# A decoder layer: gathers and loads moved, ACT in written order, last norm's scaling on ACT

## The chip, the cores and the metric

The kernel runs on one core of a Trainium2 chip. Its time is the time on the device in microseconds (us), the median of several executions. The profile is that of one execution. The engines are called TensorE (PE), VectorE (DVE), ScalarE (ACT), GpSimd (POOL) and SyncE (SP) here; SP only issues DMAs, and ACT and POOL issue some beside their other work.

## What is computed

One decoder layer on 32 sequences of 64 tokens with 512 features, all in 32-bit floats. Cut to what matters:

```python
# self-attention: 32 query heads, 8 key/value heads, head size 128
k_sel = k_cache[block_idx].reshape(-1, NKV, HD)          # 512 cached keys
k_full = concatenate([k_sel, k[0]])                      # and 64 new ones
x = layernorm(x + softmax(q @ k_full.T / sqrt(HD)) @ v_full @ wo.T)
# cross-attention: each sequence attends to its own 64 context rows
x = layernorm(x + softmax(q2 @ k2.T * scale) @ v2 @ Wo + bo)
# feed forward: z = x W + b; a low-rank m; gamma limits the norm of m
x = layernorm(x + z + min(0.5 * norm(z) / (norm(m) + 1e-6), 1) * m)
```

The 576 keys and values of the self-attention are the same for all 2048 tokens.

## The kernel before, in words

**Tiles.** The 2048 tokens form four blocks (tb) of 512. `acc[tb]` holds a block's residual, 1 MB, as four pieces of 128 tokens. The larger products (queries, output projection, keys and values of the context) are done with seven products in place of eight: the operands' quarters are first added up (`token_sums`, `output_sums`, `right_sums` on GpSimd, lines 190 to 199 and 256 to 259), and the seven results are read out of three PSUM banks x, y and z in an order given by a list. For the queries, `Queries.step(i)` issues product i on TensorE and puts the reading steps on a list: products 1 and 2 are copied by ACT (L310, L314), 6 and 7 are read by VectorE (L322, L325), and the "corner" quarter c[1, 1] is made of products 5 and 7 (L299, or L302 with a bias).

**Self-attention.** A unit n is one key/value group g, one block tb and one of that group's four heads h; there are 8 x 4 x 4 = 128 units, 16 to a group. r is the unit's number within its group. A unit has four score tiles i of 128 queries by 576 keys. For each, TensorE makes the scores (L615) in one of two PSUM buffers, VectorE takes the maximum (L620), ACT the exponential with its sum (L623), and VectorE inverts the sum (L632), scales (L633) and turns the tile in 32x32 squares (L641). `move` (L653) then rearranges the turned tiles with 16 DMAs, four for each range of 32 partitions. Two units later TensorE multiplies with the values (L661, `values` and `shared_values`), and ACT copies the result to oT (L684). Between the score tiles stand places for one query product of the next block ("q") or one output product of a past block ("w"): `steps` gives them for each h. The first blocks have an order of their own: block 1's query products come as 1, 2, 6, 5, 7, 3, 4, with z and x in the same bank.

**Around a group's change.** `load_group` loads the next group's key and value weights. `gather_keys` and `gather_values` fetch its cached rows, one indirect DMA of GpSimd each for keys and for values, four times in a group: in units r = 4, 5, 6, 7. Each is preceded by a small addition of VectorE (L538). In unit 8 `rotate` applies the rotary angles to the gathered keys: three steps on VectorE's side before the sum (L558 to L560, L562) and two on GpSimd (L557, L561). `new_keys` (matmuls L576, L582) runs in unit 8 and `cached_keys` (transposes L596) in unit 10.

**What sets the order.** A start section is written out for all engines. From there on (line 812) TensorE and VectorE run in the order in which the program names their instructions; for ACT, GpSimd and SP a scheduler of the compiler chooses the order from its own estimate of times. In the cross-attention TensorE, VectorE and GpSimd run in written order, and for the last unit and the feed forward TensorE and GpSimd only.

**Loads of the residual.** At the end of the start section (L797) the four blocks of x are loaded into `acc`, one DMA of 1 MB each, block 0 by SP and the others by ACT.

**Cross-attention.** Its 32 units are a group g and a block tb. For each, the seven query products (L282) come in the order 1, 6, 5, 7, 2, 4, 3. For the last group, g = 7, the norm of a block follows its last output product: `stats` (L149 to L152) at once, and `scale` (reciprocal L155 and four VectorE scalings L157) is put on the list `scales`, which the next unit empties after its query product 1, ahead of the reading of product 6. The list `later` holds the transposes (L129) of the scaled block; they come after query product 2. Block 2's scaling is emptied in the last pass of the loop and block 3's after it, ahead of the feed forward of block 2 (L1172 to L1206).

Of the kernel before, what the change touches and what calls it, by code (L numbers as in the profile page):

```python
# [52 lines left out]
def decoder_layer(  # L53
# [57 lines left out]
    def rows(src, tb):  # L111
        return src[tb * TB : (tb + 1) * TB, :].rearrange("(j p) f -> p j f", p=P)
# [25 lines left out]
        for part in layernorm_parts(tb, name):  # L138
            part()

    def layernorm_parts(tb, name):
        a = acc[tb]
        rstd = small.tile([P, TPB], F32, tag="rstd", name=f"rstd_{name}_{tb}")
        mv = small.tile([P, TPB, 2], F32, tag="mv", name=f"mv_{name}_{tb}")

        def stats():
            for j in range(TPB):
                st = small.tile([P, 6], F32, tag="st", name=f"st_{name}_{tb}_{j}")
                nc.vector.bn_stats(st, a[:, j, :])  # L149
                nc.vector.bn_aggr(mv[:, j, :], st)  # L150
            nc.vector.tensor_scalar_add(rstd, mv[:, :, 1], LN_EPS)
            nc.scalar.activation(rstd, rstd, AF.Sqrt)  # L152

        def scale():
            nc.vector.reciprocal(rstd, rstd)  # L155
            for j in range(TPB):
                nc.vector.tensor_scalar(  # L157
                    a[:, j, :], a[:, j, :], mv[:, j, 0:1], rstd[:, j : j + 1],
                    ALU.subtract, ALU.mult,
                )  # L160

        return stats, scale

    def layernorm_tile(tb, j, name):
        a = acc[tb][:, j, :]
# [123 lines left out]
    class Queries(Product):  # L289
        def __init__(self, left, right, qT, name, tags, bias=None):  # L290
            super().__init__(left, right, name, tags)
            self.c = {(i, j): qT[:, quarter(i, j)[0], quarter(i, j)[1]]
                      for i in range(2) for j in range(2)}
            self.bias = bias

        def final(self, y, i, j):
            c = self.c[i, j]
# [8 lines left out]
        def step(self, i):  # L306
            c = self.c
            assert not self.reads
            if i == 1:
                nc.scalar.copy(c[1, 0], self.mul("x", 1, True))  # L310
            elif i == 2:
                x = self.mul("x", 2)
                if self.bias is None:
                    nc.scalar.copy(c[0, 0], x)  # L314
                else:
                    for m in range(2):
                        nc.scalar.activation(
                            c[0, 0][:, m, :], x[:, m, :], AF.Identity, bias=self.bias[m]
                        )
            elif i == 6:  # L320
                y = self.mul("y", 6, True)
                self.reads.append(lambda: nc.vector.tensor_tensor(c[0, 1], y, c[1, 0], ALU.add))  # L322
            elif i == 7:
                y = self.mul("y", 7)
                self.reads.append(lambda: nc.vector.tensor_tensor(c[1, 1], y, c[1, 0], ALU.add))  # L325
            elif i == 4:
                y = self.mul("y", 4)
                self.reads.append(lambda: self.final(y, 1, 0))
            elif i == 5:
                z = self.mul("z", 5, True)  # L330
                self.corner = lambda: self.final(z, 1, 1)
            elif i == 3:
                z = self.mul("z", 3)
                self.reads.append(lambda: self.final(z, 0, 1))
# [129 lines left out]
    with ExitStack() as ph:  # L464
# [243 lines left out]
        def q_step(n):  # L708

            b = n // REP + 1  # L710
            if b < NB:
                if b not in qrs:

                    start_queries(b, {"x": "q", "y": "w" if b == 1 else "q", "z": "q"})
                    qrs[b].todo = list((1, 2, 6, 5, 7, 3, 4) if b == 1 else ORDER)
                i = qrs[b].todo.pop(0)
                qrs[b].step(i)
                reads.append(qrs[b].read)
                if i in (5, 7) and not {5, 7} & set(qrs[b].todo):
                    reads.append(qrs[b].corner)  # L720

        def w_step(b):
# [70 lines left out]
        nc.vector.tensor_tensor(t[4], q[1, 0], t[2], sub)  # L793
        tok[1] = token_sums(xTs[1], "tx1", nc.gpsimd)
        wo_cur[0] = load_right(woT[columns(0), :], "wo0", nc.gpsimd, first=wo_cur[0])
        for tb in range(NTB):
            (nc.scalar if tb else nc.sync).dma_start(out=acc[tb], in_=rows(x, tb))  # L797

        def last_products(i):
            if i == 3:  # L800
# [8 lines left out]

        begin.close()  # L810

        ph.enter_context(tc.manual_schedule(
            engines={mybir.EngineType.PE, mybir.EngineType.DVE}
        ))

        for n in range(N):
            b, h = divmod(n, REP)
            g, r = units[n][0], n % PER  # L820
            if r == REP and g + 1 < NKV:
                load_group(g + 1)
            if r // REP == 1 and g + 1 < NKV:
                gather_keys(g + 1, h)
            if r == 2 * REP and g + 1 < NKV:
                rotate(g + 1)
                later.append(lambda g=g: new_keys(g + 1))
            if r == 2 * REP + 1 and g + 1 < NKV:
                later.append(lambda g=g: cached_keys(g + 1))
            if n == N - REP:  # L830
                encT[0] = big.tile([P, NC, TB], F32, tag="qT", name="encT0", bufs=2)
                load_features(encT[0], encT_in, 0)
            steps = {0: "qwqw", 1: "qw q", 2: "wqwq", 3: "w qw"}[h]

            def step(place):
                if n < REP:

                    i = {(0, 0): 3, (0, 1): 7, (0, 3): 4}.get((n, place))
                    if i:
                        last_products(i)  # L840
                    elif (n, place) in ((0, 2), (1, 0), (1, 1), (1, 2), (1, 3), (2, 0), (2, 2)):
                        q_step(n)
                elif steps[place] == "q":
                    q_step(n)
                elif steps[place] == "w":
                    w_step(b - 2 if h < 2 else b - 1)
                flush()

            def spare_bank():

                if n % 2 == 0 and later:
                    later.pop(0)()

            scores(n, 0)
            step(0)
            spare_bank()
            scores(n, 1)
            if 0 < n < REP:

                move(n - 1, (3,), nc.scalar)  # L860
            if n >= 2:
                values(n - 2, 0, 2 if n % 2 == 0 else 3)
            step(1)
            scores(n, 2)
            step(2)
            if r // REP == 1 and g + 1 < NKV:
                gather_values(g + 1, h)
            scores(n, 3)
            if n >= 2:
                values(n - 2, 2 if n % 2 == 0 else 3, NKT)  # L870
                if n % 2:
                    shared_values(n - 2)
            step(3)
            spare_bank()
            if h == REP - 1:
                if b + 2 < NB:
                    g2, tb2, _ = units[(b + 2) * REP]
                    if tb2 == 0:
                        wq_cur[g2] = load_left(wqT[:, columns(g2)], f"wq{g2}", nc.gpsimd)
                    tok[b + 2] = token_sums(xTs.pop(b + 2), f"tx{g2}_{tb2}", nc.gpsimd)  # L880
                elif b + 2 == NB:
                    kvw[0] = load_kv_left(0, "wq")
                else:
                    encR[0] = token_sums(encT[0], "te0", nc.gpsimd)
            if h == REP - 1 and b + 3 < NB or n == 0:

                b2 = b + 3 if n else 2
                xTs[b2] = token_room(b2, f"xT{b2}")
                load_features(xTs[b2], xT_in, b2 % NTB)
            move(n, (0, 1, 2) if n < REP - 1 else range(NQD))  # L890

# [44 lines left out]
    with ExitStack() as ph:  # L938
# [200 lines left out]
        def project(n, *steps):  # L1139
            g, tb = units[n]  # L1140
            for i in steps:
                pjs[n].step(i)
                pjs[n].read()
            if steps[-1] == 4:
                del pjs[n]
                if g == NKV - 1:
                    stats, scale = layernorm_parts(tb, "x")
                    stats()
                    scales.append(scale)
                    later.append(lambda: transpose_block(tb, "x2"))  # L1150
# [98 lines left out]
        for n in range(N + 1):  # L1249
# [6 lines left out]
            if n < N:  # L1256
                g, tb = units[n]
                q = queries(n)
                for i in (1, 6, 5, 7):
                    q.step(i)  # L1260
                    q.read()
                    while scales:
                        scales.pop(0)()
                q.corner()
                q.step(2)


                behind = g > 0 and tb == 1
                if not behind:
                    next_tokens(n + 1, 0)  # L1270
# [102 lines left out]
```

## Time and profile before

| | |
|---|---|
| time before, median of 3 runs | 3090.13 us (3086.34 to 3092.24) |
| the profiled execution's own time | 3088.83 us |
| its span, first to last instruction | 3085.9 us |
| TensorE busy | 3034.2 us, 98% of the span |
| VectorE busy | 2186.5 us, 71% |
| ACT busy | 757.2 us, 25% |
| GpSimd busy | 967.6 us, 31% |
| TensorE's mean granted clock | 0.997 |
| self-attention | to about 1870 us |
| keys and values of the context | to about 2053 us |
| cross-attention and feed forward | to the end |

How to read the profile: a line of a timeline gives the start, the duration, the engine, the line of the kernel, the operation, what it writes and reads, how many like it were merged, and in brackets how long the engine was idle before it and what released it. A row of waits gives the engine and line that waited, what it waited for, the total in us, how many times, and the longest. Issuing a DMA is not counted as busy time; SPq, ACTq and POOLq are the issuing sequencers.

### The profile page before, as it was taken

Reading aid. Unit: us, or ns where it says so; the run is one execution under the profiler, and the core shown is the slowest. Engines: PE = TensorE matmul, PEld = TensorE weight load, DVE = VectorE, ACT = ScalarE, POOL = GpSimd, SP = SyncE. Lnnn points to the kernel's source line nnn. Section 1 sums busy time; section 2 is a strip of 40 time slices with the busy share of each in tenths; the row PEclk is TensorE's granted clock in tenths of the full one; section 3 lists DMA queues with packets and bytes.
Section 4 is the critical chain, followed back from the end, with each engine's and each line's share of the span. In section 5 each row is a group of like instructions: output and inputs, shape, how many; then the busy total and the mean of one; then the engine's idle time right before and its main releaser. Section 6 shows DMA issues by size and latency. Waiting matters only on the chain.

```text
span 3085.9 us, 42306 instructions
## 1 busy us (share of the span) xinstructions
PE 3034.2 (98%) x14944; PEld 2320.6 (75%) x14944; DVE 2186.5 (71%) x3957; ACT 757.2 (25%) x1760; POOL 967.6 (31%) x789
## 2 busy tenths in 40 slices
PE   8999999999999999999999999999999999999998
PEld 6777677777777777777777769988888888888764
DVE  6777877877877877877877764436656666666677
ACT  2323232232332232232232221211111111111122
POOL 4221322321321322322322123136444444454421
PEclk9999999999999999999999999999999999999999
DMA  6444444444444444444344343321121121121101
GB/s 210 115 115 119 113 115 122 111 122 114 109 126 115 103 129 113 106 126 115 100 125 112 96 122 138 110 96 52 52 69 49 49 69 49 49 68 49 48 28 41
DMA packets 200913, 298.66 MB, mean 97 GB/s; under 512 B 44160, under 2 KB 94848, under 8 KB 200704
## 3 DMA queue, kind: packets, MB, share of 16 engines
q1 hardware_dynamic: 187328, 282.51, 33.8%
q10 hardware_dynamic: 11328, 9.26, 1.0%
q0 software_dynamic: 2048, 4.20, 0.5%
q8 instruction: 120, 1.97, 0.3%
q14 instruction: 89, 0.73, 0.1%
HBM read 107.05 MB, written 20.97 MB: 41 GB/s over the span
## 4 chain that ended last, share of the span: by engine, by line
PE 91%; DVE 4%; DMA 2%; SPq 2%; ACT 1%; issue 1%; ACTq 0%; DVEq 0%
PE po L661 15%; PE s L615 15%; PE sx L1043 2%; PE pox L1114 2%; PE w_0y L282 1%; PE q_3y L282 1%; PE wx_2y L282 1%; PE wx_1y L282 1%; PE w_3y L282 1%; SPq L653 1%; PE qx_2y L282 1%; PE qx_3y L282 1%; PE qx_0y L282 1%; PE w_1y L282 1%; PE q_2y L282 1%; PE wx_0y L282 1%
## 5 line engine op out<-in xcount | busy, mean ns | idle before, releaser
L623 ACT ACTIVATE p<-s,nmax 128x576 f32<-128x576 f32 x512 | 380.4, 743 | 1207.7 <-DVE nmax L620 1207.6
L615 PE MATMUL s<-kT,qT 128*128 128x288 f32 x2048 | 577.9, 408 | 10.4 <-ACT p L623 9.7
L661 PE MATMUL po<-pT,v 128*128 128x512 f32 (+1 forms) x1280 | 549.2, 602 | 4.1 <-DMA pT<-T 4.1
L615 PEld LDWEIGHTS s<-kT,qT 128*128 128x128 f32 x2048 | 387.5, 190 | 115.0 <-issue 20.1
L620 DVE TENSOR_REDUCE nmax<-s 128x1 f32<-128x576 f32 x512 | 384.4, 751 | 47.6 <-PE s L615 47.1
L641 DVE STREAM_TRANSPOSE T<-p 128x576 f32<-128x576 f32 x512 | 394.5, 770 | 4.4
L661 PEld LDWEIGHTS po<-pT,v 128*128 128x128 f32 (+1 forms) x1280 | 213.7, 189 | 204.1 <-issue 177.0
L633 DVE TENSOR_SCALAR p<-p,den 128x576 f32<-128x576 f32 x512 | 324.2, 633 | 17.9
L632 DVE RECIPROCAL den<-den 128x1 f32<-128x1 f32 x512 | 84.1, 164 | 238.1 <-ACT p L623 238.1
L256 POOL TENSOR_TENSOR so<-oT,oT 128x512 f32<-128x512 f32 x32 | 42.5, 1327 | 648.5 <-ACT oT L684 648.5
L258 POOL TENSOR_TENSOR so<-oT 128x512 f32<-128x512 f32 x32 | 40.7, 1271 | 334.4 <-PE w_1y L282 93.0
L1222 POOL TENSOR_TENSOR txx<-x1T 128x512 f32<-128x512 f32 x31 | 39.5, 1275 | 229.5 <-PE qx_3z L282 93.1
L197 POOL TENSOR_TENSOR tx<-xT 128x512 f32<-128x512 f32 x31 | 39.7, 1280 | 206.6 <-PE q_3z L282 65.4
L623 ACT ACTIVATION_READ_ACCUMULATOR p<-s,nmax 128x1 f32 x512 | 99.7, 195 | 0.0
L256 POOL TENSOR_TENSOR sox<-oTx,oTx 128x512 f32<-128x512 f32 x32 | 40.5, 1267 | 184.1 <-DVE oTx L1134 178.6
L1060 ACT ACTIVATE ex<-ex 128x512 f32<-128x512 f32 x64 | 39.4, 632 | 203.2 <-DVE ex L1059 203.2
L684 ACT COPY oT<-po 128x512 f32<-128x512 f32 x128 | 72.0, 588 | 44.6 <-PE po L661 44.0
L1043 PEld LDWEIGHTS sx<-kvx,qTx 128*64 128x64 f32 x2048 | 62.3, 138 | 10.6 <-issue 10.6
L1132 ACT ACTIVATE oTx<-pox,bv 128x256 f32<-128x256 f32 x128 | 52.1, 472 | 67.6 <-PE pox L1114 67.6
L1043 PE MATMUL sx<-kvx,qTx 128*64 128x64 f32 x2048 | 66.7, 224 | 0.0
L1114 PE MATMUL pox<-pTx,kvx 64*128 64x256 f32 x512 | 64.9, 390 | 1.1 <-DMA pTx<-Tx 1.1
L1134 DVE TENSOR_SCALAR oTx<-pox,bv 128x256 f32<-128x256 f32 x128 | 53.6, 479 | 11.2 <-PE pox L1114 11.2
(445 smaller groups left out, 5778.5 us busy)
## 6 DMA issues: line engine op xcount, KB each, us to landing
pT<-T SPq DMA_DIRECT2D x1020, 80.0 KB, 2.1
pT<-T SPq DMA_DIRECT2D x1016, 64.0 KB, 2.0
xT<-in_xT SPq DMA_DIRECT2D x31, 1024.0 KB, 5.6
kvx<-kv SPq DMA_DIRECT2D x32, 512.0 KB, 3.2
pTx<-Tx SPq DMA_DIRECT2D x256, 64.0 KB, 2.0
kv<-c SPq DMA_DIRECT2D x30, 512.0 KB, 3.3
wo<-in_woT SPq DMA_DIRECT2D x32, 256.0 KB, 2.9
xwq<-in_xwq SPq DMA_DIRECT2D x32, 256.0 KB, 2.6
```

The costliest lines, as they stand in the source:

```text
L256: nc.gpsimd.tensor_tensor(t[1], a[1, 0], a[1, 1], ALU.add)
L282: nc.tensor.matmul(self.banks[b][:, m, :], self.left[i][:, k, m * P : (m + 1) * P], self.right[i][:, k, :], start=(first and m + k == 0), ...
L615: nc.tensor.matmul(s[:, a, :HALF], qTs[n // REP][:, units[n][2], i * P : (i + 1) * P], kTs[g][:, a * HALF : (a + 1) * HALF], start=True, s ...
L620: nc.vector.tensor_reduce(nmax, s[:, :, :HALF], AX.XY, ALU.max, negate=True)
L623: nc.scalar.activation(p.rearrange("q (a k) -> q a k", a=2), s[:, :, :HALF], AF.Exp, bias=nmax, accum_out=den,)
L632: nc.vector.reciprocal(den, den)
L633: nc.vector.tensor_scalar(p, p, den, None, ALU.mult)
L641: nc.vector.transpose(Ts[n][:, :, i, :], ps_.pop((n, i)).rearrange("q (b k) -> q b k", k=SQ))
L661: nc.tensor.matmul(pos[n].rearrange("d (a q) -> d a q", a=NQD), vs[units[n][0]][rows, v, :], pTs[n // 2][rows, :, chunk, :], skip_group_ch ...
L684: nc.scalar.copy(o[:, i, :].rearrange("d (t a k) -> d a t k", t=TPB, a=NQD), pos.pop(n - 1 + i).rearrange("d (a t k) -> d a t k", a=NQD, t ...
L1043: nc.tensor.matmul(s[b * SEQ : (b + 1) * SEQ, i * REP + h, :], qTs[n][:, h, pr * HF + c0 : pr * HF + c0 + SEQ], kvs[n][:, pr, 0, c0 : c0 + ...
L1114: nc.tensor.matmul(po[pr, b][:, i, :].rearrange("d (h a j) -> d h a j", h=REP, a=2), kvs[n][r, pr, 1, i * HD : (i + 1) * HD], pTs[n][r, :, ...
```

## The change

It has five parts.

1. In the self-attention ACT, too, runs in written order.
2. The gathers of the next group are in units 4, 5, 6 and 8 in place of 4 to 7, and `rotate` is in unit 9 in place of 8.
3. The residual is loaded in 16 pieces of 256 KB, one at the beginning of each of the units 1 to 16, all by ACT. The four loads of the start section are gone.
4. The fourth range of the moves is issued by ACT, one unit later, for units 0, 1, 2, 124, 125 and 126 (before: 0, 1 and 2), and block 1's product 5 is read at once (`early`), before product 7.
5. The cross-attention's last norm is scaled by ACT, as rstd * a + shift, where VectorE makes shift = -mean * rstd in one small step; and the list of scalings is emptied after the reading of query product 6.

```diff
--- before.py
+++ after.py
@@ -138,7 +138,7 @@
         for part in layernorm_parts(tb, name):
             part()
-    def layernorm_parts(tb, name):
+    def layernorm_parts(tb, name, by_act=False):
         a = acc[tb]
         rstd = small.tile([P, TPB], F32, tag="rstd", name=f"rstd_{name}_{tb}")
         mv = small.tile([P, TPB, 2], F32, tag="mv", name=f"mv_{name}_{tb}")
@@ -159,7 +159,17 @@
                     ALU.subtract, ALU.mult,
                 )
-        return stats, scale
+        def scale_by_act():
+            nc.vector.reciprocal(rstd, rstd)
+            shift = small.tile([P, TPB], F32, tag="shift", name=f"shift_{name}_{tb}")
+            nc.vector.scalar_tensor_tensor(shift, mv[:, :, 0], -1.0, rstd, ALU.mult, ALU.mult)
+            for j in range(TPB):
+                nc.scalar.activation(
+                    a[:, j, :], a[:, j, :], AF.Identity, bias=shift[:, j : j + 1],
+                    scale=rstd[:, j : j + 1],
+                )
+        return stats, scale_by_act if by_act else scale
     def layernorm_tile(tb, j, name):
         a = acc[tb][:, j, :]
@@ -292,6 +302,7 @@
             self.c = {(i, j): qT[:, quarter(i, j)[0], quarter(i, j)[1]]
                       for i in range(2) for j in range(2)}
             self.bias = bias
+            self.early = False
         def final(self, y, i, j):
             c = self.c[i, j]
@@ -322,10 +333,15 @@
                 self.reads.append(lambda: nc.vector.tensor_tensor(c[0, 1], y, c[1, 0], ALU.add))
             elif i == 7:
                 y = self.mul("y", 7)
-                self.reads.append(lambda: nc.vector.tensor_tensor(c[1, 1], y, c[1, 0], ALU.add))
+                k = c[1, 1] if self.early else c[1, 0]
+                self.reads.append(lambda: nc.vector.tensor_tensor(c[1, 1], y, k, ALU.add))
             elif i == 4:
                 y = self.mul("y", 4)
                 self.reads.append(lambda: self.final(y, 1, 0))
+            elif i == 5 and self.early:
+                z = self.mul("z", 5, True)
+                self.reads.append(lambda: nc.vector.tensor_tensor(c[1, 1], z, c[1, 0], ALU.add))
             elif i == 5:
                 z = self.mul("z", 5, True)
                 self.corner = lambda: self.final(z, 1, 1)
@@ -713,10 +729,11 @@
                     start_queries(b, {"x": "q", "y": "w" if b == 1 else "q", "z": "q"})
                     qrs[b].todo = list((1, 2, 6, 5, 7, 3, 4) if b == 1 else ORDER)
+                    qrs[b].early = b == 1
                 i = qrs[b].todo.pop(0)
                 qrs[b].step(i)
                 reads.append(qrs[b].read)
-                if i in (5, 7) and not {5, 7} & set(qrs[b].todo):
+                if i in (5, 7) and not qrs[b].early and not {5, 7} & set(qrs[b].todo):
                     reads.append(qrs[b].corner)
         def w_step(b):
@@ -793,8 +810,6 @@
         nc.vector.tensor_tensor(t[4], q[1, 0], t[2], sub)
         tok[1] = token_sums(xTs[1], "tx1", nc.gpsimd)
         wo_cur[0] = load_right(woT[columns(0), :], "wo0", nc.gpsimd, first=wo_cur[0])
-        for tb in range(NTB):
-            (nc.scalar if tb else nc.sync).dma_start(out=acc[tb], in_=rows(x, tb))
         def last_products(i):
             if i == 3:
@@ -809,23 +824,34 @@
         begin.close()
-        ph.enter_context(tc.manual_schedule(
-            engines={mybir.EngineType.PE, mybir.EngineType.DVE}
-        ))
+        ph.enter_context(tc.manual_schedule(engines={
+            mybir.EngineType.PE, mybir.EngineType.DVE, mybir.EngineType.Activation
+        }))
+        short = {0, 1, 2, *range(N - REP, N - 1)}
+        gathers = {4: 0, 5: 1, 6: 2, 8: 3}
         for n in range(N):
             b, h = divmod(n, REP)
             g, r = units[n][0], n % PER
             if r == REP and g + 1 < NKV:
                 load_group(g + 1)
-            if r // REP == 1 and g + 1 < NKV:
-                gather_keys(g + 1, h)
+            if r in gathers and g + 1 < NKV:
+                gather_keys(g + 1, gathers[r])
+            if 0 < n <= PER:
+                b2, j = divmod(n - 1, TPB)
+                nc.scalar.dma_start(out=acc[b2][:, j, :], in_=rows(x, b2)[:, j, :])
             if r == 2 * REP and g + 1 < NKV:
-                rotate(g + 1)
                 later.append(lambda g=g: new_keys(g + 1))
             if r == 2 * REP + 1 and g + 1 < NKV:
+                rotate(g + 1)
                 later.append(lambda g=g: cached_keys(g + 1))
             if n == N - REP:
                 encT[0] = big.tile([P, NC, TB], F32, tag="qT", name="encT0", bufs=2)
@@ -855,16 +881,15 @@
             step(0)
             spare_bank()
             scores(n, 1)
-            if 0 < n < REP:
+            if n - 1 in short:
                 move(n - 1, (3,), nc.scalar)
             if n >= 2:
                 values(n - 2, 0, 2 if n % 2 == 0 else 3)
             step(1)
             scores(n, 2)
             step(2)
-            if r // REP == 1 and g + 1 < NKV:
-                gather_values(g + 1, h)
+            if r in gathers and g + 1 < NKV:
+                gather_values(g + 1, gathers[r])
             scores(n, 3)
             if n >= 2:
                 values(n - 2, 2 if n % 2 == 0 else 3, NKT)
@@ -887,7 +912,7 @@
                 b2 = b + 3 if n else 2
                 xTs[b2] = token_room(b2, f"xT{b2}")
                 load_features(xTs[b2], xT_in, b2 % NTB)
-            move(n, (0, 1, 2) if n < REP - 1 else range(NQD))
+            move(n, (0, 1, 2) if n in short else range(NQD))
@@ -1144,7 +1169,7 @@
             if steps[-1] == 4:
                 del pjs[n]
                 if g == NKV - 1:
-                    stats, scale = layernorm_parts(tb, "x")
+                    stats, scale = layernorm_parts(tb, "x", by_act=True)
                     stats()
                     scales.append(scale)
                     later.append(lambda: transpose_block(tb, "x2"))
@@ -1259,7 +1284,7 @@
                 for i in (1, 6, 5, 7):
                     q.step(i)
                     q.read()
-                    while scales:
+                    while scales and i == 6:
                         scales.pop(0)()
                 q.corner()
                 q.step(2)
```

## The prediction

> **What bounds the kernel now.** I read the page first, then who waited for whom on TensorE, then the timeline round each wait of over 1 us.
>
> ```profile
> span 3085.9 us, 42306 instructions
> PE 3034.2 (98%) x14944; PEld 2320.6 (75%) x14944; DVE 2186.5 (71%) x3957; ACT 757.2 (25%) x1760; POOL 967.6 (31%) x789
> ```
>
> TensorE is the bound: it lacks work for 51.7 us of the span, and the change alters none of its matmuls. So a gain is a hole in TensorE's time, or matmuls that ran slowly after one. TensorE's waits:
>
> ```profile
> PE s L615 <- ACT p L623: 9.7, 9, 1.2
> PE po L661 <- DMA pT<-T: 4.1, 4, 2.1
> PE qx_2y L282 <- DVE qTx L322: 4.1, 1, 4.1
> PE q_1z L282 <- DVE qT L299: 3.8, 1, 3.8
> ```
>
> (Columns: total us, times, longest.) The first row is six holes of 1.21 us, one for each of the groups 1 to 6, plus 0.64, 0.70 and 1.07 elsewhere. The timeline of group 1 shows how one comes about:
>
> ```profile
> 338.60 0.95 POOL L523 DMA_INDIRECT v<-in_v_cache,row  x1 [0.30 <-issue]
> 338.89 2.97 DVE L633 TENSOR_SCALAR p<-p,den 128x576 f32<-128x576 f32 x1
> 339.57 1.27 POOL L199 TENSOR_TENSOR tx<-xT,tx 128x512 f32<-128x512 f32 x1
> 340.80 0.74 POOL L557 TENSOR_TENSOR kr<-kn,cs 128x256 f32<-128x256 f32 x1
> 343.22 0.74 ACT L623 ACTIVATE p<-s,nmax 128x576 f32<-128x576 f32 x1 [4.55 <-DVE nmax L620]
> 344.10 1.24 PE L615 MATMUL s<-kT,qT 128*128 128x288 f32 x4 [1.21 <-ACT p L623]
> ```
>
> VectorE's scaling takes 2.97 us here and mostly 0.52 us elsewhere; it ends 0.3 us after GpSimd's last of three back-to-back steps. It drags the next maximum, the exponential and the score bank. In group 0 the scaling (110.91) ends before GpSimd's tensor steps begin, and there is no hole.
>
> The last norm of block 0 in the cross-attention:
>
> ```profile
> 2902.51 3.81 DVE L157 TENSOR_SCALAR acc<-acc,mv_x,rstd_x 128x512 f32<-128x512 f32 x4
> 2906.24 0.68 DVE L322 TENSOR_TENSOR qTx<-qx_2y,qTx 128x512 f32<-128x512 f32 x1
> 2907.07 3.75 PE L282 MATMUL qx_2y<-txx,xwq 128*128 128x256 f32 x8 [4.05 <-DVE qTx L322]
> ```
>
> The scalings stand ahead of the query read that TensorE waits for. After the hole eight matmuls take 3.75 us instead of 1.89. The two iterations with transposes compare as follows (columns: stretch, its length, PE busy, granted clock, DMA share, GB/s):
>
> ```profile
> 2879.61:2918.26 38.65, 33.80 (x210) 0.91 0.10 28
> 2918.26:2949.80 31.54, 30.74 (x210) 1.00 0.13 34
> ```
>
> The same 210 matmuls cost 7.11 us more round the hole.
>
> Start and end of the self-attention:
>
> ```profile
> 46.90 0.69 DVE L299 TENSOR_TENSOR qT<-q_1z,qT 128x512 f32<-128x512 f32 x1
> 47.65 2.52 PE L282 MATMUL q_1z<-xT,wq 128*128 128x256 f32 x8 [3.84 <-DVE qT L299]
> ```
>
> ```profile
> 1821.23 3.67 PE L661 MATMUL po<-pT,v 128*128 128x512 f32 x8 [2.06 <-DMA pT<-T]
> ```
>
> In the first, product 3 waits until the corner has read product 5's bank. In the second, unit 126's weighted values wait for its rearranging DMAs.
>
> **What the Trainium skill says.** "SBUF — State Buffer", section "Who interferes with whom": GpSimd and VectorE share a port pair, a scaling of this kind can take it whole, and who comes second waits out the other's instruction. The trace agrees (2.97 against 0.52 us). "TensorE: Matmul & The Clock Gate", "What's actually happening": about 3.4 us of idleness halve TensorE's clock until some 3.4 us of work restore it. The trace agrees: after 4.05 us idle, 3.75 us for what takes 1.89; after 1.21 us idle no such slowing. "DMA: Bandwidth & Descriptors", "Issuing engines are not separate DMA queues": a second issuing engine saves only issue time. Here that is the point: 0.63 us an issue on SP's queue in the chain of waits.
>
> **The change part by part.**
>
> *Gathers at units 4, 5, 6, 8, rotation at 9.* Nothing is added: per group 8 gathers, 4 row additions and 6 rotation steps move. In unit 7 GpSimd then has only L199, which can follow L198 (ends 336.75) and end by 338.0, before the scaling at 338.89. Scaling 0.52, read, maximum at 339.9, exponential over by 341.5; TensorE wants it at 342.9. The hole goes: **6 x 1.21 = 7.3 us**. What is late next? Unit 8 takes two gathers but loses VectorE's rotation (351.41 to 353.61), and VectorE waits there for scores behind the new-key matmuls. Unit 9 gets the 2.2 us rotation; its first maximum moves from 366.5 to 368.3, its exponentials end at 369.9 and 372.9, and their banks are wanted at 373.3 and 374.3. VectorE idles 1.61 us in that unit before 373.47, plus 0.28 twice, and is level again. The rotated keys are wanted only at 381.75. Cost zero; if GpSimd held the pair once more, up to 1.2 us a group, which is the rival below.
>
> *Early corner.* The same seven products and as many reads; the read of product 5 moves ahead of product 7, so product 3 finds its bank free at about 43.7. But VectorE, busy nearly without a break from 34 to 72, sets the pace. Its own idleness that the hole caused is 1.23 + 0.46 us, and a scaling stretched to 1.50 by L199 regains about 0.7. So of 3.84 us I count **2.5** (0 to 4.5).
>
> *Loads in pieces, weights of the next group at unit 4.* Three of the four 1 MB loads leave ACT's start, one leaves SP's; 16 loads of 256 KB at units 1 to 16 take their place, each an issue of about 0.5 us on ACT between exponentials that lie 2.3 us or more apart. First needed in unit 6, the last piece of block 0 being issued in unit 4, some 28 us before. Zero; if an exponential waits in units 1 to 4, at most 0.5 each, inside the range above.
>
> *Fourth part of the moves on ACT for units 124 to 126.* Four issues each leave SP. Unit 126: 16 issues end at 1819.0 and land at 1821.0; 12 land 2.5 us sooner, when TensorE is free at 1819.2. That is 2.06 us. On ACT the four issues (2.5 us at 0.63) stand between exponentials 1 and 2 of the next unit, 2.35 us apart; behind them wait that exponential, VectorE's scaling and the next bank. I take off 0.2 for each of two units: **1.6** (0.5 to 2.1). The other move waits (1.06, 0.35) stay uncounted, because VectorE paces that stretch; so do 1.55 and 1.07.
>
> *ACT in written order.* In odd units an exponential now precedes the first oT copy (before: copy at 317.90, exponential at 318.38). The copies end near 320.1 and bank po0 is wanted at 323.2; the next score bank is wanted at 322.27, its exponential ends by 319.1. Other steps already stand in that order. Zero, with 3.1 us of cover.
>
> *Last norm on ACT behind read 6.* Read L322 can follow the statistics at 2902.05, over at 2902.7; product 5 keeps TensorE to 2902.86. So the hole and its slow matmuls go: 7.1, less 0.1: **7.0** (4.0 to 7.1). Added per block: one small VectorE step (0.2) and four ACT steps, 128x512 with two pointer operands. This trace has none; the nearest is 0.63 (L1060), and "ScalarE: Activation LUTs", "What ACT_TABLE_LOAD costs", gives 186 + 0.833 x 512 + 2 x 93 = 0.80 us, an estimate. At 0.80 they end by 2906.5; the transposes start near 2906.3 and take column blocks in turn, so no wait; at 0.63 still less. For block 3, VectorE's four scalings (1.92) leave the chain ahead of uT: TensorE's 0.63 us hole at 3034.22 closes. **0.7** (0 to 1.0).
>
> Sum: 7.3 + 2.5 + 1.6 + 7.0 + 0.7 = 19.1. The profiled execution took 3088.83 us (2.9 round its span); less 19.1 gives 3069.7, say **3070**. Its time is 1.3 below the median of the three runs, inside their spread of 5.9.
>
> **Rivals.** *The boundary hole only moves* to unit 8 or 9: 7.3 us less gain, 3077. For it: GpSimd and VectorE still meet there. Against: the slack worked out above. *Only the norm counts*: ACT's order is what it was, and start and boundary are paced by VectorE; 7.7 us, 3081. For it: VectorE's density up to 72 us; against: group 0 without a hole. *Slower*: ACT in order stops at a copy or an issue while a ready exponential queues behind it, in every pair of units. It decides once that costs more than the 3.1 us of cover. At 0.6 us beyond it, 62 pairs lose 37 us: 3107. Against: ACT is 25% busy and already runs nearly in this order.
>
> **Numbers.** 3070: 0.68; 3077: 0.14; 3081: 0.11; 3107: 0.07. The upper ends sum to 21.8 (3067), and runs scatter by 3, so the low end is 3064; the high end takes in the second rival, 3082. About 0.2% (6 us) is what a measurement can tell from no change. The 3081 case is close to that line, so half of it goes to "same": faster 0.87, same 0.06, slower 0.07.
>
> **What would show it.** No 2.97 us scaling in unit 7 and no 1.21 us rows; no wait of qx_2y for L322 and a clock of 1.00 there; q_1z waiting under 1 us but rows "s <- ACT p" still near 60 us; the 2.06 us row gone; the two-unit step of 27.97 us unchanged. A longer step, or a new hole in units 8 to 10, would make the prediction wrong.

## The result and the profile after

The changed kernel takes 3067.14 us (median; 3065.60 to 3067.85) where the kernel before, run beside it, took 3090.16 (3086.34 to 3092.24): ratio 0.9927, 95% interval 0.9918 to 0.9937, a gain of 22.6 us (19.5 to 25.3) by the ratio, 23.0 between the medians. The forecast was 3070, range 3064 to 3082. The profiled execution took 3067.85 us with a span of 3066.1, against 3088.83 and 3085.9 before.

The head of the page after, and its longest rows of who waited for whom on TensorE (total us, times, longest):

```profile
span 3066.1 us, 42299 instructions
PE 3028.1 (99%) x14944; PEld 2317.9 (76%) x14944; DVE 2171.1 (71%) x3945; ACT 766.4 (25%) x1776; POOL 961.1 (31%) x789
```

```profile
PE po L677 <- DMA pT<-T: 6.0, 4, 1.8
PE q_0x L292 <- DMA xT<-in_xT: 5.0, 1, 5.0
PE s L631 <- ACT p L639: 4.2, 5, 1.7
```

(The added lines shift the numbers: scores L631, exponential L639, scaling L649, values L677.) TensorE lacks work for 38.0 us, before 51.7. The rows of qx_2y and q_1z are gone; the row "s <- ACT p" has halved, and none of its five holes, 1.70 us at the longest, is at a group's change. The timeline of group 1's change, unit 7:

```profile
334.90 1.27 POOL L209 TENSOR_TENSOR tx<-xT,tx 128x512 f32<-128x512 f32 x1
336.90 0.52 DVE L649 TENSOR_SCALAR p<-p,den 128x576 f32<-128x576 f32 x1
339.08 1.89 PE L292 MATMUL q_2z<-xT,wq 128*128 128x256 f32 x8
340.81 1.13 PE L631 MATMUL s<-kT,qT 128*128 128x288 f32 x4
341.77 2.08 PE L677 MATMUL po<-pT,v 128*128 128x512 f32 x6
```

GpSimd is done 0.7 us before the scaling, which takes 0.52 us instead of 2.97, and no bracket stands behind the scores. The last norm of block 0, and its iteration of 210 matmuls (stretch, length, busy time and instructions of PE, its weight loads, VectorE, ACT and GpSimd, then granted clock, DMA share, GB/s):

```profile
2889.76 0.69 DVE L333 TENSOR_TENSOR qTx<-qx_2y,qTx 128x512 f32<-128x512 f32 x1
2890.67 1.89 PE L292 MATMUL qx_2y<-txx,xwq 128*128 128x256 f32 x8
2890.76 2.93 ACT L167 ACTIVATE acc<-acc,shift_x,rstd_x 128x512 f32<-128x512 f32 x4 [0.67 <-DVE shift_x L165]
```

```profile
2867.43:2898.98 31.55, 30.75 (x210) 26.10 (x210) 23.07 (x45) 9.75 (x17) 13.74 (x11) 1.00 0.12 34
```

The read stands ahead of the scalings, eight matmuls take 1.89 us instead of 3.75, and the iteration takes 31.55 us instead of 38.65. What is left of the end of the self-attention:

```profile
1789.88 1.96 PE L677 MATMUL po<-pT,v 128*128 128x512 f32 x4 [1.82 <-DMA pT<-T]
1810.33 3.70 PE L677 MATMUL po<-pT,v 128*128 128x512 f32 x8 [0.39 <-ACT oT L700]
```

The 2.06 us hole has shrunk to 0.39, but another, of 0.35 us before, is now 1.82 in this profile.

Both kernels do the same matmuls, so the places of TensorE at the same piece of work give the gain by stretch:

| stretch, by TensorE's place before | before | after | gained |
|---|---|---|---|
| start to the new keys of group 1 (123.98) | 123.98 | 122.06 | 1.9 |
| groups 1 to 6, to the new keys of group 7 (1490.44) | 1366.46 | 1359.95 | 6.5 |
| end of the self-attention, to the second context tile (1860.43) | 369.99 | 367.54 | 2.5 |
| to the last group's first norm (2876.07) | 1015.64 | 1014.34 | 1.3 |
| that norm's iteration (2967.85) | 91.78 | 84.68 | 7.1 |
| to the last pu (3054.91) | 87.06 | 85.76 | 1.3 |
| to the end of the span | 31.04 | 31.74 | -0.7 |

The rows add up to 19.9 us, the difference of the spans. The profiles of the experiments show which rows repeat. The 1.3 us up to the norm come and go with kernels that don't touch that part (a wait for pTx in the profile before, 1.06 us, that most others lack). Groups 1 to 6 gain 8.6, 8.8, 8.9, 8.6, 7.5 and 7.7 us in the six other kernels with the gathers and the rotation moved (e1, e4, e5, e6, e7, e12): this profile lost some 2 us that don't repeat, 1.46 of them in one wait for pT at 876.62 that five of those six lack.

### The profile page after: what moved, and what is told of

It reads as the page before. It is cut to its first block, busy times and chain, and to the rows that moved or that the text cites. A ratio compares the mean times of both kernels' runs of the same rounds, so it can differ in the third digit from the quotient of the medians.

```text
span 3066.1 us, 42299 instructions
## 1 busy us (share of the span) xinstructions
PE 3028.1 (99%) x14944; PEld 2317.9 (76%) x14944; DVE 2171.1 (71%) x3945; ACT 766.4 (25%) x1776; POOL 961.1 (31%) x789
## 4 chain that ended last, share of the span: by engine, by line
PE 91%; DVE 4%; SPq 2%; DMA 1%; ACT 1%; issue 1%; ACTq 0%; DVEq 0%
PE po L677 15%; PE s L631 14%; PE sx L1068 2%; PE pox L1139 2%; SPq L669 2%; PE wx_2y L292 1%; PE w_0y L292 1%; PE wx_1y L292 1%; PE wx_0y L292 1%; PE w_3y L292 1%; PE qx_3y L292 1%; PE qx_2y L292 1%; PE qx_0y L292 1%; PE q_2y L292 1%; PE wx_3y L292 1%; PE qx_1y L292 1%
## 5 line engine op out<-in xcount | busy, mean ns | idle before, releaser
L639 ACT ACTIVATE p<-s,nmax 128x576 f32<-128x576 f32 x512 | 379.1, 741 | 1244.9 <-DVE nmax L636 1234.8
L631 PE MATMUL s<-kT,qT 128*128 128x288 f32 x2048 | 576.5, 407 | 5.0 <-ACT p L639 4.2
L677 PE MATMUL po<-pT,v 128*128 128x512 f32 (+1 forms) x1280 | 549.0, 602 | 6.4 <-DMA pT<-T 6.0
L631 PEld LDWEIGHTS s<-kT,qT 128*128 128x128 f32 x2048 | 387.2, 190 | 108.0 <-issue 18.7
L677 PEld LDWEIGHTS po<-pT,v 128*128 128x128 f32 (+1 forms) x1280 | 213.3, 189 | 206.5 <-issue 177.8
L649 DVE TENSOR_SCALAR p<-p,den 128x576 f32<-128x576 f32 x512 | 319.9, 625 | 17.9
L639 ACT ACTIVATION_READ_ACCUMULATOR p<-s,nmax 128x1 f32 x512 | 98.7, 193 | 0.0
```

The costliest lines, as they stand in the source:

```text
L631: nc.tensor.matmul(s[:, a, :HALF], qTs[n // REP][:, units[n][2], i * P : (i + 1) * P], kTs[g][:, a * HALF : (a + 1) * HALF], start=True, s ...
L639: nc.scalar.activation(p.rearrange("q (a k) -> q a k", a=2), s[:, :, :HALF], AF.Exp, bias=nmax, accum_out=den,)
L649: nc.vector.tensor_scalar(p, p, den, None, ALU.mult)
L677: nc.tensor.matmul(pos[n].rearrange("d (a q) -> d a q", a=NQD), vs[units[n][0]][rows, v, :], pTs[n // 2][rows, :, chunk, :], skip_group_ch ...
```

## The experiments

All times are medians, with the kernel before run on the same chip; "lead" is how much earlier TensorE is at the same place than in the profile of the kernel before. A gain named in the text is the difference of the two medians; the ratio is an estimate of its own and gives up to 1.4 us more or less.

| kernel | us | before beside it | ratio, 95% interval |
|---|---|---|---|
| e1 gathers and rotation alone | 3080.38 | 3089.34 | 0.9968 [0.9957, 0.9980] |
| e8 rotation alone | 3089.38 | 3089.34 | 1.0000 [0.9991, 1.0008] |
| e10 one product on VectorE | 3084.14 | 3088.35 | 0.9986 [0.9979, 0.9992] |
| e11 two gathers in unit 6 | 3082.90 | 3088.35 | 0.9982 [0.9974, 0.9989] |
| e2 norm alone | 3080.78 | 3089.34 | 0.9968 [0.9956, 0.9980] |
| e3 norm's order alone | 3083.55 | 3089.34 | 0.9979 [0.9970, 0.9989] |
| e9 ACT's order alone | 3086.71 | 3088.35 | 0.9995 [0.9987, 1.0003] |
| e4 changed, ACT's order free | 3079.76 | 3088.33 | 0.9972 [0.9962, 0.9983] |
| e5 changed, no early corner | 3069.78 | 3088.33 | 0.9939 [0.9925, 0.9952] |
| e6 changed, loads at the start | 3066.12 | 3088.33 | 0.9925 [0.9911, 0.9938] |
| e7 changed, last moves on SP | 3068.16 | 3088.33 | 0.9934 [0.9920, 0.9947] |
| e12 changed, other moves on ACT | 3067.71 | 3088.35 | 0.9930 [0.9917, 0.9944] |

### What made the holes at the group's change

**e1** is the kernel before with part 2 of the change alone.

```diff
+        gathers = {4: 0, 5: 1, 6: 2, 8: 3}
-            if r // REP == 1 and g + 1 < NKV:
-                gather_keys(g + 1, h)
+            if r in gathers and g + 1 < NKV:
+                gather_keys(g + 1, gathers[r])
...
-                rotate(g + 1)
                 later.append(lambda g=g: new_keys(g + 1))
...
+                rotate(g + 1)
                 later.append(lambda g=g: cached_keys(g + 1))
```

> The kernel before with only the gathers moved to units 4, 5, 6 and 8 and the rotation to unit 9. My theory (GpSimd's work in unit 7 holds the port pair while VectorE scales): no scaling above 1.6 us in the last stretch of unit 7, the six 1.21 us holes gone, 7 to 9 us faster, about 3082. Rival (the conflict only moves to units 8 and 9): within 1 us of the kernel before, with a new hole in unit 8 or 9. Rival (most of the gain comes from ACT's written order, not from the gathers): the holes shrink but stay.

It gained 9.0 us, and its lead grew by 8.6 us over groups 1 to 6. The holes are gone, and none came up in units 8 to 10: the theory holds, and so does the claim that unit 8 and 9 take the moved work at no cost. But a hole of 1.21 us was worth more than 1.21. From q_2z to the values two steps on, TensorE took 4.18 us with the hole (341.00 to 345.18) and 2.69 without (339.08 to 341.77). A merged row reaches 0.16 us into the next one where work is queued (339.08 + 1.89 is 340.97, and the scores start at 340.81); a stall loses that too, and the step after it starts its successor 0.11 later. So 1.21 + 0.16 + 0.11 is 1.48, and six of them 8.9.

**e8** moves only the rotation, **e10** only its first product.

```diff
-            nc.gpsimd.tensor_tensor(k4[:, :, :, 1], o, c3, ALU.mult)
+            (nc.vector if g else nc.gpsimd).tensor_tensor(k4[:, :, :, 1], o, c3, ALU.mult)
```

> The kernel before with only the rotation moved from unit 8 to unit 9; the gathers stay in units 4 to 7. Theory (the scaling of 2.97 us waits for the tensor operations of GpSimd's queue, L199 and then the rotation's first product of 0.74 us): the scaling shrinks to about 2.2 us, the hole from 1.21 to about 0.5, some 4 us faster, about 3086. Rival (the two gathers of unit 7, which push L199 behind them, are all that counts): the scaling stays at 2.97 and the time within 1 us.

> The kernel before with the rotation's first product (L557, 0.74 us on GpSimd) on VectorE; gathers and rotation stay in their units. It runs directly after L199 on GpSimd, whatever unit it is written in. Theory (it is the second half of what the 2.97 us scaling waits for): the scaling shrinks to about 2.2 us, the six 1.21 us holes to about 0.5, some 4 us faster, about 3085. Rival (L199 alone holds the scaling): holes unchanged, within 1 us. Rival (the gathers' descriptor work holds it too): unchanged as well.

e8 changed nothing, and not for the reason of its rival. Its timeline in unit 7:

```profile
339.87 2.96 DVE L633 TENSOR_SCALAR p<-p,den 128x576 f32<-128x576 f32 x1
340.54 1.27 POOL L199 TENSOR_TENSOR tx<-xT,tx 128x512 f32<-128x512 f32 x1
341.76 0.74 POOL L557 TENSOR_TENSOR kr<-kn,cs 128x256 f32<-128x256 f32 x1
```

The rotation is written in unit 9, but its first product runs where GpSimd's queue has got to, directly behind L199: the edit moved VectorE's steps and not GpSimd's. My expectation had overlooked that. e10 takes the product away from GpSimd:

```profile
339.96 2.28 DVE L633 TENSOR_SCALAR p<-p,den 128x576 f32<-128x576 f32 x1
340.64 1.27 POOL L199 TENSOR_TENSOR tx<-xT,tx 128x512 f32<-128x512 f32 x1
344.48 1.24 PE L615 MATMUL s<-kT,qT 128*128 128x288 f32 x4 [0.52 <-ACT p L623]
```

The scaling loses 0.68 us, all six holes 0.69, and the kernel gains 4.2 us: the scaling had been waiting for both GpSimd steps. In both kernels it starts 0.68 us ahead of L199, while a gather still runs, and ends 0.3 us after GpSimd's last step.

**e11** leaves the rotation in unit 8 and pulls the fourth gathers into unit 6.

```diff
+        parts_of = {4: (0,), 5: (1,), 6: (2, 3)}
-            if r // REP == 1 and g + 1 < NKV:
-                gather_keys(g + 1, h)
+            for t in parts_of.get(r, ()) if g + 1 < NKV else ():
+                gather_keys(g + 1, t)
```

> The kernel before with the fourth key and value gathers pulled into unit 6 beside the third (units 4, 5, 6, 6), the rotation left in unit 8. GpSimd's L199 of unit 7 then follows L198 at once, as in the changed kernel, and the rotation's first product follows L199. Theory (all that matters is that no gather stands between L198 and L199, so that GpSimd is done before the scaling): holes gone or below 0.4, 6 to 8 us faster, about 3081. Rival (unit 8 is needed for the fourth gather, or the rotation in unit 9): the holes stay or move to unit 6, gain below 3 us.

The holes of unit 7 are gone and the lead grew by 6.7 us, though the median's gain is 5.5. One thing went otherwise than expected: the rotation's product runs in unit 6, directly behind the last gather (331.36), and there a scaling of 1.95 us (331.70) waits for it and the next step, at no idle time of TensorE. So what counts is that GpSimd is done before the scaling of unit 7; unit 8 is one place of several for the gathers. The lead grows 0.3 us a group less than in e1. Four gathers in a row push the sums of the output weights: in all six groups TensorE's weight loads now wait for them (3.4 us in all), and in one TensorE itself idles for more than a tenth of a microsecond.

```profile
789.74 1.99 PE L282 MATMUL w_0y<-wo,so 128*128 128x256 f32 x8 [0.46 <-POOL wo L198]
```

### The last norm: the order or the engine?

**e2** is the kernel before with part 5 alone; **e3** changes only the place.

```diff
                     q.read()
-                    while scales:
+                    while scales and i == 6:
                         scales.pop(0)()
```

> The kernel before with only the last norm's scaling on ACT, behind the query read. Theory: the 4.05 us hole ahead of qx_2y and the slow matmuls after it go, 7 us; block 3's 0.63 us hole ahead of the last feed-forward goes, 0.7 us: 7 to 8 us faster, about 3082. Rival (most of it comes back, because ACT now holds the transposes back): 2 us or less.

> The kernel before with only the place of the last norm's scalings changed: still on VectorE, but behind the read of query product 6 instead of ahead of it. If the order alone removes the hole (the read no longer stands behind four scalings): 5 to 7 us faster with no hole ahead of qx_2y, ACT adding only the 0.7 us at block 3. If the engine is what counts (the scalings then hold up the next reads, of products 5 and 7, instead): a hole of 1 to 4 us moves to the next matmuls, 0 to 5 us faster.

e2 gained 8.6 us: 7.1 in the norm's iteration and 1.3 up to the last pu. e3 gained 5.8, with 6.3 and 0.4 in the same places. So order is most of it. The two medians lie 2.8 us apart, but their intervals overlap, so the engine's part rests on the traces: 0.8 in the iteration, where the stretched scalings hold VectorE and so its copy of a transpose (TensorE waits 1.2 us for x1T, in e2 0.3), and 0.9 at block 3. The line of e3:

```profile
2903.58 4.77 DVE L157 TENSOR_SCALAR acc<-acc,mv_x,rstd_x 128x512 f32<-128x512 f32 x4
```

### ACT in written order

**e9** is the kernel before with ACT added to the written order and nothing else; **e4** is the changed kernel with ACT taken out of it.

```diff
-            engines={mybir.EngineType.PE, mybir.EngineType.DVE}
+            engines={mybir.EngineType.PE, mybir.EngineType.DVE, mybir.EngineType.Activation}
```

> The kernel before with one edit: ACT joins TensorE and VectorE in the written order of the self-attention, everything else as before. Theory (the order has value only for loads and moves that hang on nothing, which the scheduler would hoist; here the acc loads are still in the start section): within 2 us of the kernel before. Rival (the order by itself frees the start and the end of the self-attention): 2 to 5 us faster, first new keys of group 1 before 123 and the w_2x hole of 1.0 to 1.5 us gone. Rival of the forecast (a copy or an issue in order holds up exponentials in every pair of units): slower by more than 6 us, a two-unit step above 27.97.

> The changed kernel with ACT left to the scheduler again in the self-attention; PE and VectorE stay as written. Theory (ACT's written order costs and gains nothing): within 1.5 us of the changed kernel, some 3067, groups 1 to 6 gaining 1.47 us each against the kernel before. Rival (the written order costs: the changed kernel's groups 1 to 6 gained 6.5 us where the kernel with the gathers alone gained 8.6): 2 us faster than the changed kernel, all of it in those groups. Rival (the written order gains, by early copies): slower than 3069, with new small holes 's <- ACT p'.

e9 is the same as the kernel before: from group 1 to the second context tile its lead stays between 0.25 and -0.30 us, and the slower rival is out. e4 fits none of the three expectations as a whole. Groups 1 to 6 gain 8.8 us, as its theory had it, but of the change's gain only 8.6 us are left, and not because of new small holes. ACT's timeline at its start (merged rows of ACTq are issues), then TensorE's:

```profile
9.33 0.33 ACTq L850 DMA_DIRECT2D acc<-in_x  x1
9.69 1.28 ACT L321 ACT_TABLE_LOAD   x1 [9.69 <-DMA acc<-in_x]
10.99 0.58 ACT L321 COPY qT<-q_0x 128x512 f32<-128x512 f32 x1
12.05 4.99 ACTq L850 DMA_DIRECT2D acc<-in_x  x3
17.09 0.58 ACT L325 COPY qT<-q_0x 128x512 f32<-128x512 f32 x1 [5.51 <-DMA wv<-in_wvT]
```

```profile
11.62 3.78 PE L292 MATMUL q_0x<-xT,wq 128*128 128x256 f32 x8 [3.10 <-ACT qT L321]
26.20 1.62 PE L631 MATMUL s<-kT,qT 128*128 128x288 f32 x4 [3.71 <-issue]
1784.07 4.86 PE L677 MATMUL po<-pT,v 128*128 128x512 f32 x6 [5.30 <-DMA pT<-T]
```

Free to choose, the scheduler pulls the pieces of x, which wait for nothing, ahead of the copies that TensorE needs; the first three, issued between 2.83 and 9.66, stand ahead of the first copy. The new keys of group 1 come at 128.70, 6.6 us after the changed kernel's. At the end of the self-attention it loses 6.3 more, 5.3 in one wait for pT: SP's 16 issues there take 14.18 us instead of 10.01, 4.1 of it a wait at the fifteenth. That issue waits on a semaphore on which a move issued by ACT also counts; ACT issued it at 1778.94, after waiting for VectorE's turned tile, it landed at 1780.94, and SP went on at 1780.95. (3.1 us more of this profile's loss lie in the last pu, where the clock fell.) So the written order gains nothing by itself, and the pieces on ACT need it. For the moves on ACT no run separates the order from the pieces.

### The start, and the loads

**e5** is the changed kernel without `early`; **e6** has the four loads of 1 MB back at the end of the start section.

```diff
-                    qrs[b].early = b == 1
```

```diff
+        for tb in range(NTB):
+            (nc.scalar if tb else nc.sync).dma_start(out=acc[tb], in_=rows(x, tb))
...
-            if 0 < n <= PER:
-                b2, j = divmod(n - 1, TPB)
-                nc.scalar.dma_start(out=acc[b2][:, j, :], in_=rows(x, b2)[:, j, :])
```

> The changed kernel without the early corner of block 1. Theory (the corner ahead of product 7 is what gains at the start): q_1z waits some 3.8 us for the read again, the first new keys of group 1 come 2 to 3 us later than in the changed kernel (122.06), the whole 2 to 3 us slower, about 3069.5. Rival (VectorE or the loads pace the start): the hole is back and the new keys come within 0.7 us of 122.06.

> The changed kernel with the four 1 MB loads of acc at the start section again, in place of the 16 pieces. Theory (worth nothing): new keys of group 1 within 0.5 us of 122.06, 3067. Rival (the early loads compete with the operands of the start, and the pieces are what frees the start): new keys 1 to 3 us later. Rival (the 16 issues between exponentials cost): 0.5 to 2 us faster.

The intervals overlap, so the place of group 1's new keys has to tell. Six profiles with the old start (e1, e2, e3, e8, e10, e11) have them between 124.95 and 125.51, the kernel before at 123.98, an early one. Four with the early corner and ACT's order (e6, e7, the changed kernel, e12) have them at 121.10, 121.72, 122.06 and 123.57. So the new start is worth about 3 us, a median of 121.9 against 125.05 for the seven. e5, with the corner late, has them at 123.33, and its hole is back:

```profile
46.31 3.40 PE L292 MATMUL q_1z<-xT,wq 128*128 128x256 f32 x8 [3.84 <-DVE qT L310]
```

By these places the corner gives 1.4 us, but the profiles differ by a microsecond or more before the corner comes. From the scores just ahead of q_1z (at 42.67 in the profile before) to the new keys it is 79.5 to 79.9 us in those four, 82.0 in e5 and 81.1 to 82.3 in the seven old starts. So the corner gives 1.5 to 2.2 us of its 3.84 us hole. The rest comes back as waits for exponentials: four rows "s <- ACT p" between 48 and 64 us hold 3.79 us in the changed kernel, two hold 1.34 in e5. What else the new start gains lies ahead of the corner. Between 34 and 43 us TensorE waits 0.8 to 2.5 us in each of the six old starts, and not in the six profiles with ACT in written order (e9 among them); but the profile before has no such wait either, so that order as the cause is not shown. e6, at 121.10, shows no cost of the loads at the start and none of the pieces.

### The moves at the end

**e7** keeps all issues of units 124 to 126 on SP; **e12** was meant as a better kernel.

```diff
-        short = {0, 1, 2, *range(N - REP, N - 1)}
+        short = {0, 1, 2}
```

```diff
-        short = {0, 1, 2, *range(N - REP, N - 1)}
+        short = {0, 1, 2, 3, N - 5, N - 3, N - 2}
```

> The changed kernel with all 16 issues of the moves of units 124 to 126 on SP's queue again. Theory (1.6 us from the last move): the 2.06 us hole 'po <- pT' near 1821 in the kernel before is back and that of 1.82 us near 1790 shrinks to 0.35; from the last new keys (1482) to the first kv_1x (1850) 1 to 2.5 us longer than in the changed kernel, in all 1 to 2.5 us slower, about 3069. Rival (the four issues on ACT cost as much as SP's gain): within 0.7 us.

> The changed kernel with the fourth part of the move on ACT for units 0 to 3, 123, 125 and 126 instead of 0 to 2 and 124 to 126: the two units whose pT is awaited by TensorE at 82.96 (1.39 us) and 1775.80 (1.35 us) are added, and 124, whose hole grew from 0.35 to 1.82, is taken out. Theory (SP's 16 issues a unit set these holes): 1 to 3 us faster than the changed kernel, about 3065. Rival (VectorE and the exponentials pace both stretches): within 0.7 us of it, each hole's place taken by one named for ACT's p.

In e7 the hole of 2.1 us is back, and the stretch to the second context tile is 1.1 us longer than in the changed kernel. The hole near 1790, which I had put down to ACT's issues, is 1.24 us there and named for ACT's p, and 1.37 in e9: it goes with ACT's written order. It does not go with the issues, since e5 and e6 have them on ACT too and wait 1.28; the 1.82 of the changed kernel's profile does not repeat. e12 is no faster, and no run gave a kernel that beats the changed one beyond its interval. The waits for pT that it was aimed at gave way to exponentials:

```profile
87.98 1.24 PE L631 MATMUL s<-kT,qT 128*128 128x288 f32 x4 [1.00 <-ACT p L639]
1788.67 1.96 PE L677 MATMUL po<-pT,v 128*128 128x512 f32 x4 [0.99 <-ACT p L639]
```

So the rival holds: VectorE and ACT pace these stretches, and a move that lands earlier only changes whom TensorE waits for.

## Why the prediction was right

The time fell inside the range, 2.9 us under the forecast, and each of the five terms is there. With the values that repeat over the profiles (for groups 1 to 6 the median of seven, for the start the two medians above) the sum is 8.6 + 3.1 + 2.5 + 7.1 + 1.3 = 22.6 us, against 19.1 predicted and 22.6 measured. That the last two agree so well is chance: single terms scatter by about 1 us, and the sum leaves out the last stretch, in which the changed kernel, e5, e6, e7 and e12 lost 0.2 to 2.4 us. The two-unit step, named as a sign, is mostly 27.97 us in both profiles. The upper ends of the prediction's terms add up to 22.0 rather than 21.8, on which nothing hangs.

- **Gathers and rotation, 7.3.** Mechanism right, size too small: 8.6. The term took the printed idle time, 1.21 us, for the cost of a hole; it is 1.48. Unit 8 and 9 cost nothing, as worked out. The prediction did not say which of the two moves empties GpSimd's unit 7; by e8 and e11 it is the gathers' alone.
- **Early corner, 2.5.** The whole start gains about 3, the corner 1.5 to 2.2 of it. The mechanism is right: the holes "s <- ACT p" near 60 us grew in place of the corner's (1.70 at 57.98), as VectorE's pace there implies. The rest lies ahead of the corner; it may go with ACT's order, which I had at nothing, but that is not shown.
- **Loads in pieces, 0.** Right, by e6, but only under the written order: e4 prices the same pieces without it.
- **Moves at the end, 1.6.** e7 gives 1.1, inside the bounds. The stretch as a whole gained 2.5 in the profiled run; no run shows where the rest comes from. The w_2x hole of 1.55, which I left uncounted, is gone there, but in e9, where ACT's order alone shrinks it to 0.39, the one of 0.35 grows to 1.37 and the stretch gains nothing.
- **ACT in written order, 0.** Right for what it was: e9 finds -0.05% (-0.13 to +0.03%). What the step did not say is that part 3 leans on it.
- **Last norm, 7.0 and 0.7.** 7.1 and 1.3. The change of order alone makes 6.3 of the 7.1. At block 3, 0.4 of the 1.3 lie ahead of pu of block 1, where I had looked for nothing. The new ACT step lasts 0.803 us on average over 16, for the estimate of 0.80 from the Trainium skill, "ScalarE: Activation LUTs", "What ACT_TABLE_LOAD costs".

The two smaller-gain rivals are out by e1, in which the boundary's holes go for good, and the slower one by e9.

## What to carry to other kernels

A printed hole is not its price. The boundary's 1.21 us cost 1.48; of the start's 3.84 at most 2.2 came back, and the w_2x hole's 1.16 in e9 brought nothing, because other waits grew. Before adding up holes, compare the distance between the same two steps with and without one. When a step is moved to free a shared resource, look for where the other engine's queue will really run it: an instruction runs when its queue reaches it and its operands are there, not where it is written. An order written by hand can be worth nothing alone and still be what makes the next change pay, so test a set of edits by taking one out as well as by putting one in.

## What the runs showed of the hardware

- In unit 7 VectorE's scaling waited for two GpSimd steps in a row: it takes 0.52 us alone, 2.28 where e10 leaves the one step of 1.27, and 2.97 with one of 0.74 behind that. The Trainium skill, "SBUF — State Buffer", "Who interferes with whom", speaks of the other's whole instruction; here it was two. That is no rule for steps without a gap. In the 14 profiles 300 scalings met two such steps, and 263 of them ended within 0.45 us of the first step's end, while the second ran, as this one of e11 does. What lets VectorE in is open.

```profile
323.62 1.27 POOL L196 TENSOR_TENSOR tx<-xT 128x512 f32<-128x512 f32 x1
324.52 0.69 DVE L633 TENSOR_SCALAR p<-p,den 128x576 f32<-128x576 f32 x1
324.85 1.49 POOL L259 TENSOR_TENSOR so<-oT,so 128x512 f32<-128x512 f32 x1
```

- A gather's descriptor work alone holds the scaling little or not at all. In the changed kernel the two below run together at full speed; scalings that start 0.6 us after a gather's start take 0.61 us and end 0.3 us after it (six in the profile before). What holds the 2.97 us scaling in its first 0.68 us, beside a gather and before L199 starts, is open.

```profile
348.62 0.94 POOL L539 DMA_INDIRECT v<-in_v_cache,row  x1 [0.30 <-issue]
348.91 0.52 DVE L649 TENSOR_SCALAR p<-p,den 128x576 f32<-128x576 f32 x1
```

- The same eight matmuls of the last pu, after an idle 1.07 to 1.11 us and then 1.76 to 1.83, took 3.67 us in seven profiles, 5.37 in six and 6.72 in one. So TensorE's clock can fall after far less than the 3.4 us of idleness that the prediction quoted from "TensorE: Matmul & The Clock Gate". The place of the pause in time decides. In each profile the granted clock changes only at multiples of 3.41 us from one another. Cut into intervals on that grid, the 14 profiles have 42 after which the clock fell from full to half, 14 of them at the kernel's end; TensorE was busy for less than 47% of every one of the 42. Of the 12468 after which it stayed, one is below 46%. The pause of 3.9 to 4.0 us began 1.05 to 2.28 us after a grid point in the seven fast cases, and 2.28 to 2.88 us or 0.16 us after one in the slow ones.
